# A kernel's first microseconds: fewer zeros, another order of loads and scales, identities scaled in place of weights

## The chip, the cores and the metric

The kernel runs on one core of one Trainium2 chip. A core has five engines that run beside each other and wait for each other by semaphores: TensorE (PE, matmuls; its weight loads are shown apart as PEld), VectorE (DVE), ScalarE (ACT), GpSimd (POOL), and SyncE (SP), which here only issues transfers. ScalarE can issue transfers too. Data lie in SBUF, 128 partitions wide; matmuls write to PSUM, from where VectorE and ScalarE read. The metric is the device time of one execution in microseconds, as a median of several runs. The profiler records one further execution, instruction by instruction; times in it are counted from the start of its span.

## The reference, cut to what matters

Four convolution layers over a signal of 128 samples, 64 channels and 1024 positions, each with weights that are scaled per sample ("modulated") and normalised ("demodulated"). The second layer upsamples and blurs, the fourth blurs and downsamples. The result is added to the input.

```python
CIN, COUT, K, STYLE_DIM = (64, 64, 3, 128)
TYPES = ('same', 'upsample', 'same', 'downsample')
SCALE = 1.0 / sqrt(CIN * K ** 2);  EPS = 1e-08
BLUR_K = [1, 3, 3, 1] / 8

def _layer(x, style, w, b, mw, mb, typ):
    s = style @ mw.T + mb
    weight = SCALE * w * s[:, None, :, None]
    demod = rsqrt(sum(weight * weight, axis=(2, 3)) + EPS)
    weight = weight * demod[:, :, None, None]
    if typ == 'same':       out = conv_same(x, weight) + b
    elif typ == 'upsample': out = blur(conv_up(x, weight) + b, 2 * BLUR_K, (1, 1))
    elif typ == 'downsample': out = conv_down(blur(x, BLUR_K, (2, 2)), weight) + b
    return out

out = x
for i, typ in enumerate(TYPES):
    out = _layer(out, style, weights[i], biases[i], mod_w[i], mod_b[i], typ)
return x + out
```

## The kernel before, in words

All numbers are 32-bit floats. No layer is run over the signal by itself. For every sample the four layers are folded into one filter of nine taps (64 x 64 channels each), and this filter is run over the input. Samples are treated four at a time, a *quad*; there are 32 quads, two samples in the upper and two in the lower 64 partitions. The filter of a quad is made by TensorE in three stages: stage 1 (`stage1`, L410; matmuls by `tap_matmul`, L392) multiplies w2 with w3, scaled per sample (the tiles `wd`, made by `scale3`); stage 2 (`stage2`; matmuls at L553 or L470) multiplies that with E, the blurred w1; stage 3 (L585) multiplies with w0. Between the stages ScalarE or VectorE copy PSUM to SBUF and scale by tables per sample: `S` by tB after stage 1, `R` by tC after stage 2, `Wf` by t0 after stage 3. Then the convolutions over the input run (`product`, L767); their sums are scaled to outputs and stored.

The order of the instructions is written out by hand: each engine executes its instructions in the order in which the program names them, and waits where an operand isn't ready. The scheduler is off. A short prologue, from L1135 on, comes ahead of the loop over quads, and its order is what is changed.

What the prologue does. The parameters come in two arrays: `par_s` with the modulation weights, the styles and the biases, in two parts (the first has layers 2 and 3 and the first 16 samples; the second has layers 0 and 1 and the other samples), and `par` with the weights of the convolutions, copied into the upper and the lower 64 partitions (`HALF`). `par` begins with w2 (KC = 192 columns), then w1 reversed (`w1r`) and a 64 x 64 identity (`idn`), 256 columns together, up to `cuts[1]`; then w3 and w2 in another order up to `cuts[2]`; then the rest. SyncE issues all transfers but two, which ScalarE issues. A transfer is issued in the order of its queue. Behind the parameters, SyncE issues the input of quad 0 (`load(0)`, tile X).

VectorE sets a tile Z to zero, and TensorE multiplies zeros into the two banks of the PSUM tile Y (`zeros_to_y`, L183). These banks are opened that way, and the blur of w1 adds to them. Then `mod_matmul` (L207) multiplies styles with the modulation weights, `mod_scale` (L213) makes `sc`, the scale of each sample and channel, `mod_square` its square `ssq`, `q2_sum` (L228, L229) the sum of the squared weights over taps, and `var_matmul` (L235) the sum under the root. `var_root` (L248, L252) takes the reciprocal root on ScalarE and the sum on VectorE; `newton` (L258 to L260) refines the root in three operations on VectorE. This is done first for layer 2 (`first_inverse`, giving `d2`), which `table_A` needs for the table tA that scales `wd`, and later for all layers (`rest_of_scales`, giving `dm`, from which tC is made).

The blur of w1: `blur_scale` (L320) makes four scaled copies of w1 in the tile `w1s` on ScalarE, one for each distinct value of the seven blur coefficients; `blur_matmul` (L339) multiplies them with the identity and adds them, shifted, into Y; there are 18 matmuls in five steps, taps with 192, 192, 192, 128 and 64 columns in the longer of the two halves. `blur_copy` (L352) copies Y to E.

`load`, `in_g01`, `in_g2`, `in1`, `in2`, `in3` and `in04` (VectorE or GpSimd) form sums and differences of the input. `weight_sums`, `scaled_weights` and the tables tB and t0 run on GpSimd. `ps_conv`, `ps_w` and `ps_y` are the PSUM pools; the modulation's tiles psM lie in `ps_conv`, and the second quad's stage 1 takes the place of the first of them.

Of the kernel before, what the change touches and what calls it, by code (L numbers as in the profile page):

```python
# [63 lines left out]
def kernel(  # L64
# [46 lines left out]
    nc.scalar.dma_start(par[T, :KC], params[:, :KC])  # L111
    nc.sync.dma_start(par_s[:, PS:], params_s[:, PS:])
    nc.scalar.dma_start(par[Bo, : cuts[1]], params[:, : cuts[1]])
    nc.sync.dma_start(par[T, KC : cuts[1]], params[:, KC : cuts[1]])
    for i, j in zip(cuts[1:], cuts[2:]):
        for rows in HALF:
            nc.sync.dma_start(par[rows, i:j], params[:, i:j])
# [32 lines left out]
    Z = const.tile([P, 384], F32, name="Z")  # L150
    E = const.tile([P, NT, C], F32, name="E")
    w1s = const.tile([P, K + 1, K, C], F32, name="w1s")
    nc_v.memset(one, 1.0)
    nc_v.memset(Z[:, :256], 0.0)
    nc_v.memset(Z[:, 256:], 0.0)
# [3 lines left out]
    load(0)  # L159

# [16 lines left out]
    def zeros_to_y(sets, n, start=True):  # L177


        for i in range(sets):  # L180
            rows = HALF[i % 2]
            for cols in HALF:
                nc.tensor.matmul(  # L183
                    Y[cols, i % 2, :n],
                    Z[rows, :C],
                    Z[rows, :n],
                    start=start,
                    stop=True,
                    skip_group_check=not start,
                )  # L190
# [35 lines left out]

    def q2_sum(ls):
# [34 lines left out]
    def first_inverse(bs, src):  # L262

        var_root(bs, src, slice(2, 3), d2[:, None], nc_v)
        newton(var[:, 2, bs], d2, n2)
# [52 lines left out]
    def blur_scale(ks):  # L318
        for i in ks:
            nc_a.activation(w1s[:, i], w1r, AF.Copy, scale=BLUR2[i])  # L320

    def blur_matmul(ps, ks):
# [10 lines left out]
        for k in ks:  # L333
            for r, rows in enumerate(HALF):
# [3 lines left out]
                for cols in HALF:  # L338
                    nc.tensor.matmul(  # L339
                        ps[r][cols, C * (i - lo) : C * (j - lo)],  # L340
                        idn[rows],
                        w1s[rows, min(b, n - 1 - b), i - b : j - b],
# [795 lines left out]
    zeros_to_y(2, 96, False)  # L1138
    nc_v.tensor_scalar_mul(mbs, mb, SCALE)
    mod_matmul(first, pm[0][0], (2, 3))  # L1140
    nc_a.activation(wsq[T, 2], wio[2][T], AF.Square)
    blur_scale(range(2))
    mod_matmul(first, pm[1][0], (0, 1))
    zeros_to_y(2, 128, False)
    mod_scale(first, pm[0][0], slice(2, 4))
    mod_square(first, L2)
    q2_sum(L2)
    var_matmul(first, pm[0][1], (2,))
    mod_scale(first, pm[1][0], L01)
    mod_square(first, L01)  # L1150
    mod_square(first, L3)
    table_B(first)
    table_0(first)
    first_inverse(first, pm[0][1])
    blur_scale(range(2, 4))
    nc_a.activation(wsq[T, 3], wio[3][T], AF.Square)
    blur_matmul(psB, range(5))
    table_A(first, d2)
    scale3(0, BOTH)
# [13 lines left out]
    in_g01(0, PAIR[0])  # L1173
    scale3(1)
    scale3(2)

    def rest_of_scales():
        var_root(first, pm[0][1], eng=nc_v)
# [477 lines left out]
```

## Time and profile before

| | |
|---|---|
| median of 3 runs | 478.26 us (476.77 to 479.97) |
| the profiled execution | 477.31 us, its span 475.5 us |
| granted TensorE clock in it | 0.998 |
| TensorE busy | 469.0 us, 99% of the span |
| VectorE, ScalarE, GpSimd busy | 418.3, 310.6, 163.2 us |
| first zero matmul, first load of the blur, of stage 1, of stage 2 | 1.36, 5.10, 7.51, 10.28 us |

How to read it. In the timeline a line gives the start in us, the length, the engine, the line of the program, the operation, output and inputs, and how many instructions of that kind were merged; behind it, in brackets, how long the engine was idle before and what ended that. `x16` at TensorE counts two records for each matmul of 32-bit floats. In the chain of work that ended last each step is followed back to what released it. Queues are marked with a q (SPq, ACTq). A mean over the 475 us says nothing of the first 14; these are read from the timeline.

### The profile page before, as it was taken

To read this page: it belongs to the slowest core of one execution; us is meant where nothing else is said; L and a number is where in the kernel's file an instruction comes from. 1 tells how busy PE (TensorE), PEld (TensorE's weight loads), DVE (VectorE), ACT (ScalarE), POOL (GpSimd) and SP (SyncE) were. 2 spreads that over 40 slices of the span, in tenths; PEclk is the share of its full clock that TensorE was granted. 3 is DMA by queue.
4 is the path that set the end of the run, shared out by engine and by line. 5 is a ranking of instruction groups with operands and counts; after the bars stand their busy time and mean duration, and the time that the engine had idled before them with its cause. 6 is when DMAs were issued, how large, how long until landed. Compare 5 with 4: busy or idle time off the path is not lost.

```text
span 475.5 us, 26756 instructions
## 1 busy us (share of the span) xinstructions
PE 469.0 (99%) x11928; PEld 351.4 (74%) x11928; DVE 418.3 (88%) x693; ACT 310.6 (65%) x709; POOL 163.2 (34%) x197
## 2 busy tenths in 40 slices
PE   8999999999999999999999999999999999999996
PEld 7986788776778877677776677766777788767863
DVE  4889998879989998999979899979999999999895
ACT  5475666668766676766657666667666768766443
POOL 3534032663534342233432233422334432333200
PEclk9999999999999999999999999999999999999999
DMA  5237455545445554345553455544555554455125
GB/s 176 78 108 222 152 160 170 152 132 167 142 139 174 153 177 127 126 145 174 158 156 128 124 167 152 174 128 125 149 175 157 165 157 144 145 145 176 64 91 193
DMA packets 52243, 70.71 MB, mean 149 GB/s; under 512 B 5856, under 2 KB 49824, under 8 KB 52128
## 3 DMA queue, kind: packets, MB, share of 16 engines
q1 hardware_dynamic: 51536, 68.32, 46.4%
q8 instruction: 93, 1.52, 1.4%
q10 hardware_dynamic: 592, 0.69, 0.5%
q14 instruction: 22, 0.18, 0.1%
HBM read 35.36 MB, written 33.62 MB: 145 GB/s over the span
## 4 chain that ended last, share of the span: by engine, by line
PE 94%; DVE 4%; issue 1%; ACT 0%; ACTq 0%; DVEq 0%
PE psA L767 45%; PE Y L767 11%; PE psR L470 9%; PE psA L585 7%; PE psW L585 7%; PE psS L392 5%; PE psR L553 4%; PE psA L470 2%; PE Y L1008 2%; PE Y L339 1%; DVE H L676 1%; PE Y L183 1%; DVE T L754 1%; DVE G L676 0%; PE psM L207 0%
## 5 line engine op out<-in xcount | busy, mean ns | idle before, releaser
L767 PE MATMUL psA<-T,H 64*64 64x340 f32 x2304 | 186.1, 446 | 0.2 <-DVE y L676 0.2
L767 PEld LDWEIGHTS psA<-T,H 64*64 64x64 f32 x2304 | 91.5, 133 | 46.7 <-issue 2.1
L676 DVE SCALAR_TENSOR_TENSOR G<-X 128x1376 f32<-128x1376 f32 (+2 forms) x65 | 78.4, 1212 | 0.2
L740 POOL TENSOR_TENSOR T<-G 128x684 f32<-128x684 f32 x28 | 46.5, 1659 | 74.1 <-DVE G L676 74.1
L448 POOL TENSOR_TENSOR S<-S 128x128 f32<-128x128 f32 x28 | 21.8, 778 | 139.5 <-ACT S L363 132.2
L363 ACT ACTIVATE R<-psR,tC 128x448 f32<-128x448 f32 x63 | 36.6, 631 | 44.7 <-PE psR L470 26.5
L767 PE MATMUL psA<-T,Wf 64*64 64x340 f32 x768 | 64.0, 446 | 0.0
L767 PE MATMUL Y<-T,Wf 64*64 64x340 f32 x768 | 62.6, 451 | 0.1
L676 DVE SCALAR_TENSOR_TENSOR Y<-m,psA 128x340 f32<-128x340 f32 x64 | 33.0, 516 | 27.6 <-PE psA L767 26.2
L363 ACT ACTIVATE psW<-psA 128x128 f32<-128x128 f32 x100 | 19.3, 268 | 49.2 <-PE psA L585 45.1
L754 DVE TENSOR_TENSOR T<-G 128x1368 f32<-128x1368 f32 (+1 forms) x33 | 50.8, 1541 | 0.0
L363 ACT ACTIVATE Wf<-psW,t 128x256 f32<-128x256 f32 (+2 forms) x76 | 32.7, 480 | 26.5 <-PE psW L585 25.6
L725 DVE TENSOR_TENSOR T<-X 128x684 f32<-128x684 f32 x32 | 48.4, 1513 | 0.0
L470 PE MATMUL psR<-S,E 64*64 64x64 f32 (+1 forms) x1472 | 46.9, 237 | 0.0
L745 POOL TENSOR_TENSOR T<-G 128x684 f32<-128x684 f32 x28 | 46.5, 1660 | 0.0
L392 PEld LDWEIGHTS psS<-wd,w2n 64*64 64x64 f32 x1120 | 34.6, 133 | 12.9
L470 PEld LDWEIGHTS psR<-S,E 64*64 64x64 f32 x1472 | 39.5, 134 | 4.9 <-ACT psR L493 0.2
L767 PEld LDWEIGHTS Y<-T,Wf 64*64 64x64 f32 x768 | 30.2, 132 | 17.1 <-DVE Y L676 0.6
L844 ACT ACTIVATE o<-psA,tb,td 128x340 f32<-128x340 f32 x63 | 37.1, 648 | 6.3 <-PE psA L767 6.3
L767 PEld LDWEIGHTS psA<-T,Wf 64*64 64x64 f32 x768 | 30.2, 133 | 13.9
L844 ACT ACTIVATE o<-Y,tb,td 128x340 f32<-128x340 f32 x63 | 36.7, 639 | 4.5 <-PE Y L767 2.7
L844 ACT ACTIVATE o<-y,tb,td 128x340 f32<-128x340 f32 x62 | 38.6, 679 | 0.6 <-DVE y L826 0.6
(165 smaller groups left out, 832.9 us busy)
## 6 DMA issues: line engine op xcount, KB each, us to landing
out<-o SPq DMA_DIRECT2D x185, 170.0 KB, 2.8
X<-in_x SPq DMA_DIRECT2D x150, 172.0 KB, 3.5
X<-in_x SPq DMA_DIRECT2D x14, 516.0 KB, 5.0
out<-o SPq DMA_DIRECT2D x2, 340.0 KB, 2.8
Xe<-in_x_ends SPq DMA_DIRECT2D x1, 512.0 KB, 5.2
out<-o ACTq DMA_DIRECT2D x3, 170.0 KB, 2.7
par<-in_params SPq DMA_DIRECT2D x2, 192.0 KB, 3.6
par<-in_params SPq DMA_DIRECT2D x2, 96.0 KB, 2.6
```

Source lines behind the costliest of these rows:

```text
L363: nc_a.activation(dst, src, AF.Copy, scale=f)
L392: nc.tensor.matmul(ps[r][cols, at * C : (at + n) * C], weight[rows], wd[c if r == 0 else 1 - c][rows, taps], start=first, stop=last, skip_ ...
L448: nc_g.tensor_add(t[:, :, 2], t[:, :, 2], t[:, :, 0])
L470: nc.tensor.matmul(dst[r][cols], weight[rows], st[c if r == 0 else 1 - c][rows, slots, :], start=False, stop=last, skip_group_check=True,)
L585: nc.tensor.matmul(dst[r][cols], weight[rows], t[rows, c, slots, :], start=first, stop=last, skip_group_check=True,)
L676: nc_v.scalar_tensor_tensor(out, x, f, y, op0=ALU.mult, op1=op)
L725: nc_v.tensor_sub(t[:, pairs, 0, :NJ], plane(X, 3, pairs), plane(X, 1, pairs))
L740: eng.tensor_add(t[:, :, 0, :NJ], plane(g, 2), plane(g, 1))
L745: eng.tensor_sub(t[:, :, 1, :NJ], plane(g, 2), plane(g, 1))
L754: nc_v.tensor_sub(t[:, pairs, :, :NJ], both(a, PL), both(b, 1))
L767: nc.tensor.matmul(ps[s][cols, :NB], w, Ts[q, tag][rows, c, i, g : g + NB], start=(g == 0 and m == 3), stop=(g == K - 1), skip_group_check ...
L844: nc_a.activation(dst, src, AF.Identity, bias=add, scale=d3)
```

## The change

Five things, all in the prologue.

- The transfers: w1 and the identity go second and third in SyncE's queue, both halves; then w3 and the other w2; then the second part of `par_s`; then the rest. ScalarE issues only the upper half of w2. The lower half of w2 goes behind the input of quad 0.
- Z has 64 columns instead of 384 and is set first; the zero matmuls read it repeatedly. The second set of zeros has 128 columns instead of 96.
- The modulation matmuls of layer 2, layer 3 and layers 0 and 1 go in three calls; layer 2's scale is made by itself, and its sum of squared weights by one reduction (`q2_first`). Layers 0 and 1 go between the second and the third step of the blur. `newton_of` reads the sum from PSUM and adds EPS within its first operation.
- The blur multiplies w1 by four scaled identities (`idb`, 64 columns each, made by VectorE) instead of scaled copies of w1 by an identity.
- The roots of all layers, their Newton steps and tC come directly behind quad 0's S, ahead of `wd` of quads 1 and 2 and of quad 0's `in_g01`; `var` is made after them (`first_var`).

```diff
     nc.scalar.dma_start(par[T, :KC], params[:, :KC])
+    for rows in HALF:
+        nc.sync.dma_start(par[rows, KC : cuts[1]], params[:, KC : cuts[1]])
+    for rows in HALF:
+        nc.sync.dma_start(par[rows, cuts[1] : cuts[2]], params[:, cuts[1] : cuts[2]])
     nc.sync.dma_start(par_s[:, PS:], params_s[:, PS:])
-    nc.scalar.dma_start(par[Bo, : cuts[1]], params[:, : cuts[1]])
-    nc.sync.dma_start(par[T, KC : cuts[1]], params[:, KC : cuts[1]])
-    for i, j in zip(cuts[1:], cuts[2:]):
-        for rows in HALF:
-            nc.sync.dma_start(par[rows, i:j], params[:, i:j])
+    for rows in HALF:
+        nc.sync.dma_start(par[rows, cuts[2] :], params[:, cuts[2] :])
...
-    Z = const.tile([P, 384], F32, name="Z")
+    Z = const.tile([P, C], F32, name="Z")
     E = const.tile([P, NT, C], F32, name="E")
-    w1s = const.tile([P, K + 1, K, C], F32, name="w1s")
+    idb = const.tile([P, K + 1, C], F32, name="idb")
+    nc_v.memset(Z, 0.0)
     nc_v.memset(one, 1.0)
-    nc_v.memset(Z[:, :256], 0.0)
-    nc_v.memset(Z[:, 256:], 0.0)
     nc_v.memset(eps, EPS)
 
     nc_a.activation(one, one, AF.Abs_reciprocal_sqrt)
     load(0)
+    nc.sync.dma_start(par[Bo, :KC], params[:, :KC])
...
-                    Y[cols, i % 2, :n],
-                    Z[rows, :C],
-                    Z[rows, :n],
+                    Y[cols, i % 2, :n].rearrange("c (a o) -> c a o", o=C),
+                    Z[rows],
+                    Z[rows, None, :].to_broadcast([C, n // C, C]),
...
+    def q2_first():
+        nc_v.tensor_reduce(
+            q2[T, 2],
+            wsq[T, 2].rearrange("i k o -> i o k"),
+            axis=mybir.AxisListType.X,
+            op=ALU.add,
+        )
...
-    def first_inverse(bs, src):
-
-        var_root(bs, src, slice(2, 3), d2[:, None], nc_v)
-        newton(var[:, 2, bs], d2, n2)
+    def newton_of(src, y, n):
+        nc_v.scalar_tensor_tensor(n, src, EPS, y, op0=ALU.add, op1=ALU.mult)
+        nc_v.scalar_tensor_tensor(n, n, -0.5, y, op0=ALU.mult, op1=ALU.mult)
+        nc_v.scalar_tensor_tensor(y, n, 1.5, y, op0=ALU.add, op1=ALU.mult)
+
+    def first_inverse(bs, ps, ls, y, n):
+
+        src = by_layer(ps, bs)[:, ls]
+        nc_a.activation(y, src, AF.Abs_reciprocal_sqrt, bias=eps)
+        newton_of(src, y, n)
+
+    def first_var(bs, ps):
+        nc_v.tensor_scalar(var[:, :, bs], by_layer(ps, bs), EPS, None, op0=ALU.add)
...
-    def blur_scale(ks):
-        for i in ks:
-            nc_a.activation(w1s[:, i], w1r, AF.Copy, scale=BLUR2[i])
+    def blur_scale():
+        for i in range(K + 1):
+            nc_v.tensor_scalar(idb[:, i], idn, BLUR2[i], None, op0=ALU.mult)
...
-                        idn[rows],
-                        w1s[rows, min(b, n - 1 - b), i - b : j - b],
+                        idb[rows, min(b, n - 1 - b)],
+                        w1r[rows, i - b : j - b],
...
     zeros_to_y(2, 384)
-    zeros_to_y(2, 96, False)
+    zeros_to_y(2, 128, False)
     nc_v.tensor_scalar_mul(mbs, mb, SCALE)
-    mod_matmul(first, pm[0][0], (2, 3))
+    mod_matmul(first, pm[0][0], (2,))
+    mod_matmul(first, pm[1][0], (3,))
     nc_a.activation(wsq[T, 2], wio[2][T], AF.Square)
-    blur_scale(range(2))
+    zeros_to_y(2, 128, False)
+    mod_scale(first, pm[0][0], L2)
+    mod_square(first, L2)
+    q2_first()
+    var_matmul(first, pm[0][1], (2,))
+    mod_scale(first, pm[1][0], L3)
+    blur_scale()
+    blur_matmul(psB, range(2))
     mod_matmul(first, pm[1][0], (0, 1))
-    zeros_to_y(2, 128, False)
-    mod_scale(first, pm[0][0], slice(2, 4))
-    mod_square(first, L2)
-    q2_sum(L2)
-    var_matmul(first, pm[0][1], (2,))
+    blur_matmul(psB, range(2, 5))
+    first_inverse(first, pm[0][1], L2, d2[:, None], n2[:, None])
+    table_A(first, d2)
+    scale3(0, BOTH)
     mod_scale(first, pm[1][0], L01)
+    table_B(first)
+    table_0(first)
     mod_square(first, L01)
     mod_square(first, L3)
-    table_B(first)
-    table_0(first)
-    first_inverse(first, pm[0][1])
-    blur_scale(range(2, 4))
     nc_a.activation(wsq[T, 3], wio[3][T], AF.Square)
-    blur_matmul(psB, range(5))
-    table_A(first, d2)
-    scale3(0, BOTH)
     for l in range(2):
         nc_a.activation(wsq[T, l], wio[l][T], AF.Square)
     blur_copy(psB, (nc_a, nc_a))
...
     stage1(0, None, BOTH, rest_of_var)
-    in_g01(0, PAIR[0])
+    first_inverse(first, pm[0][1], slice(0, NL), dm[:, :, first], nw[:, :, first])
+    table_C(first, nc_v)
     scale3(1)
     scale3(2)
-
-    def rest_of_scales():
-        var_root(first, pm[0][1], eng=nc_v)
-        var_newton(first)
-        table_C(first, nc_v)
-
-    stage2(0, None, BOTH, rest_of_scales)
+    first_var(first, pm[0][1])
+    in_g01(0, PAIR[0])
+    stage2(0, None, BOTH)
```

## The prediction, made before the changed kernel ran

> **What bounds the kernel now.** First the page of the profile: the span, the busy shares, the granted clock by slices, and the chain that ended last by engines.
>
> ```profile
> span 475.5 us, 26756 instructions
> ## 1 busy us (share of the span) xinstructions
> PE 469.0 (99%) x11928; PEld 351.4 (74%) x11928; DVE 418.3 (88%) x693; ACT 310.6 (65%) x709; POOL 163.2 (34%) x197
> ...
> PEclk9999999999999999999999999999999999999999
> ...
> PE 94%; DVE 4%; issue 1%; ACT 0%; ACTq 0%; DVEq 0%
> ```
>
> TensorE (PE) is busy 99% of the span and is 94% of the chain. What the change does to other engines counts only where it moves the moment at which TensorE gets its next work. All edits lie in the first 14 us. So the second view is the timeline of that stretch, TensorE's weight loads alone (start, length, line, count): where a group starts, its matmuls could go.
>
> ```profile
> 1.35 0.30 PEld L183 LDWEIGHTS Y<-Z 64*64 64x64 f32 x8 [1.35 <-DVE eps L156]
> 2.05 0.25 PEld L183 LDWEIGHTS Y<-Z 64*64 64x64 f32 x4 [0.39 <-issue]
> 2.69 0.25 PEld L183 LDWEIGHTS Y<-Z 64*64 64x64 f32 x4 [0.39 <-issue]
> 3.16 0.93 PEld L207 LDWEIGHTS psM<-par_s 128*64 128x64 f32 x16 [0.22 <-issue]
> 4.13 0.31 PEld L183 LDWEIGHTS Y<-Z 64*64 64x64 f32 x8
> 4.66 0.29 PEld L235 LDWEIGHTS psM<-ssq,q 64*64 64x64 f32 x4 [0.22 <-DVE q L229]
> 5.10 2.64 PEld L339 LDWEIGHTS Y<-w1s,par 64*64 64x64 f32 x36
> 7.51 1.86 PEld L392 LDWEIGHTS psS<-wd,par 64*64 64x64 f32 x48
> 9.29 0.43 PEld L235 LDWEIGHTS psM<-ssq,q 64*64 64x64 f32 x12
> 9.75 0.39 PEld L207 LDWEIGHTS psM<-par_s 128*64 128x64 f32 x8
> 10.28 2.42 PEld L553 LDWEIGHTS psR<-S,E 64*64 64x64 f32 x72
> 12.97 0.39 PEld L207 LDWEIGHTS psM<-par_s 128*64 128x64 f32 x8 [0.28 <-issue]
> 13.51 1.09 PEld L392 LDWEIGHTS psS<-wd,par 64*64 64x64 f32 x48
> ```
>
> Read downwards: zero matmuls (L183), the modulation (L207), the sum of squares of layer 2 (L235), the blur of w1 (L339), the first quad's stage 1 (L392), its stage 2 (L553), the second quad's stage 1. From 5.10 on one group follows the other. The blur takes 7.51 - 5.10 = 2.41 us and sets the start of stage 1. Two more facts stand here. Before the blur there are holes, and the modulation lies in them. And the same 48 loads of L392 take 1.86 us at 7.51 but 1.09 at 13.51: TensorE is slow at first, though the granted clock is full.
>
> Third, what releases the blur and stage 1: ScalarE's timeline.
>
> ```profile
> 4.68 0.61 ACT L320 ACTIVATE w1s<-par 128x192 f32<-128x192 f32 x2 [0.96 <-DMA par<-in_params]
> 5.21 0.26 ACT L248 ACTIVATE d<-psM,eps 128x16 f32<-128x16 f32 x1
> ...
> 6.70 0.46 ACT L363 ACTIVATE wd<-par,tA 128x192 f32<-128x192 f32 x1 [0.48 <-DVE tA L290]
> ...
> 11.43 0.30 ACT L248 ACTIVATE dm<-psM,eps 128x64 f32<-128x64 f32 x1
> 13.23 0.64 ACT L363 ACTIVATE R<-psR,tC 128x448 f32<-128x448 f32 x1 [1.50 <-DVE tC L290]
> ```
>
> The blur waits for w1: ScalarE idles 0.96 us on the transfer until 4.68, then scales. Stage 1's weights wd are done at 6.70 + 0.46 = 7.16, which is 0.35 before TensorE is through the blur. So the blur starts stage 1, not the chain of d, tA and wd. Last, SyncE's queue (SPq) and the view of the DMAs (KB each, us from issue to landing).
>
> ```profile
> 0.73 0.38 SPq L110 DMA_DIRECT2D par_s<-in_params_s  x1
> 1.17 0.42 SPq L112 DMA_DIRECT2D par_s<-in_params_s  x1
> 1.63 0.57 SPq L114 DMA_DIRECT2D par<-in_params  x1
> 2.25 2.53 SPq L117 DMA_DIRECT2D par<-in_params  x4
> 4.83 15.99 SPq L146 DMA_DIRECT2D X<-in_x  x4
> ```
>
> ```profile
> par<-in_params SPq DMA_DIRECT2D x2, 96.0 KB, 2.6
> ...
> par_s<-in_params_s SPq DMA_DIRECT2D x1, 120.0 KB, 2.3
> par<-in_params ACTq DMA_DIRECT2D x1, 112.0 KB, 2.8
> par_s<-in_params_s SPq DMA_DIRECT2D x1, 76.0 KB, 1.9
> par<-in_params SPq DMA_DIRECT2D x1, 64.0 KB, 3.0
> ```
>
> w1's upper half is the 64 KB: 1.63 + 3.0 = 4.63, the last to land ahead of 4.68.
>
> **The change, part by part.**
>
> *Fewer zeros.*
>
> ```profile
> 0.80 0.06 DVE L153 MEMSET one<- 128x1 f32 x1 [0.80 <-PEq L1637]
> 0.89 0.27 DVE L154 MEMSET Z<- 128x256 f32 x1
> ```
>
> The new memset of 64 columns costs between nothing and this 0.27; a quarter of the columns would be 0.07 and there is some fixed cost, so I take 0.12. Z now comes first, at 0.80, so TensorE starts near 0.97 instead of 1.35. Its second set of zeros grows from 96 to 128 columns; 384 columns took 2.69 - 1.41 = 1.28, so 32 more are at most 0.1; I take 0.05. The modulation stood behind the zeros, not behind its data (par_s landed at 0.73 + 1.9 = 2.63), so it goes from 3.16 to about 2.83.
>
> *Layer 2's scale first.* The first scale needs two matmuls fewer: 16 loads go in pairs in 0.93, about 0.1 a pair, so with the 0.33 it comes some 0.5 earlier. Two additions for q2 become one reduction, which the trace doesn't show. Its bounds are 0.26 and 0.46, by d (16 columns) and wd (192, as many as it reads), both ScalarE's; I take 0.33, nearer to the short one, as it has half the partitions. The sum of squares starts near 4.0 instead of 4.66, and d near 4.45 instead of 5.21. Newton loses one of four operations. But the four identities stand ahead of Newton on VectorE: behind their wait for w1 queue Newton, tA, half of wd, and the scale of layers 0 and 1.
>
> *w1 and the identities.* SyncE now issues: par_s part one at 0.73; w1's upper half at 1.17; its lower half 0.57 and a gap of 0.05 later at 1.79; w3's two half rows at 2.41 and 3.03; par_s part two at 3.66; the rest; X of quad 0 near 5.4; w2's lower half. The upper half lands by 1.17 + 3.0 = 4.17. The lower half lands between 1.79 + 1.9 = 3.7 and 1.79 + 3.0 = 4.8; I take 4.4, by the 2.6 of the 96 KB in the same queue. The scaling of an identity has 64 columns; w1s took 0.61 for two of 192, so one identity lies between 0.1 and 0.3, and I take 0.2. The blur starts near 4.65, 0.45 earlier. The four identities end near 5.0, Newton, tA and wd follow and end near 6.5, so wd is still not what stage 1 waits for.
>
> The lower half left ScalarE's queue, which issued it beside SyncE's transfers, and is now issued in series. [...]
>
> *What is put into the blur.* The modulation of layers 0 and 1 lay in the hole ahead of the blur and cost nothing. Now it stands between the blur's second and third tap, and needs par_s part two, which is issued at 3.66 instead of 1.17. It lands at 3.66 + 2.3 = 5.96, between 5.6 (1.9) and 6.7 (3.0). In the longer of the blur's halves the taps have 192, 192, 192, 128 and 64 columns, so the first two are half of it, 1.2 us: they end at 4.65 + 1.2 = 5.85. TensorE waits until 5.96. The detour itself: from L207's first load at 3.16 to the next group's at 4.13 are 0.97 for eight pairs of loads; with four pairs 0.57, and with the 0.22 idle ahead of them 0.79. The wait covers that 0.22 here, so 0.57 counts. The blur's other half is 1.2 again: stage 1 starts at 5.96 + 0.57 + 1.2 = 7.73 instead of 7.51. **So 0.45 is gained in front of the blur and about 0.67 is paid inside it: 0.2 later.** An earlier w1 helps no further, since par_s part two is the floor.
>
> *Roots ahead of wd.* dm follows S on ScalarE instead of four wd, so it moves from 11.43 to about 10.3, and tC with it. R's idle of 1.50 on tC shrinks, but that is ScalarE's. R ended at 13.23 + 0.64 = 13.87, while TensorE had the second quad's stage 1 until 13.51 + 1.09 = 14.6. It gains nothing. wd of quads 1 and 2 comes about 0.4 later, near 12, and is wanted at 13.51: no cost.
>
> *The rest.* X is issued 0.6 later; its first user on VectorE now stands behind tC, near 12, 7 us after the issue. The squares of layers 0 and 1 wait for a transfer that is issued 0.6 later, and are wanted by L235 at 9.29 and after. w2's lower half is wanted by GpSimd after stage 2. I cost these at nothing; if the squares' cover fails, the 9.29 group and stage 2 move by up to those 0.6.
>
> **Sum.** Stage 1 starts 0.2 later. If TensorE's change to the quick pace stays where it is, between 7.5 and 10.3, a later stage 1 has more of its loads in the quick time and gives about half back. I take +0.1 on the profiled execution's 477.31 (span 475.5 and 1.8 around it). The median of the three runs, 478.26, is 0.95 above that execution, so the forecast is 478.4, in effect no change. The runs spread from 476.77 to 479.97; about 1% is what a measurement of this kernel can tell from no change.
>
> **Rivals.**
>
> *Quick pace sooner (faster).* TensorE gets dense work 0.4 earlier, and the pace may change before stage 1 or even the blur. Stage 1 at the quick pace saves 1.86 - 1.09 = 0.77, the blur by the same ratio 2.41 x 0.41 = 1.0; at most 1.8, and 1.4 with the 0.2 lost and half of a blur slow: 477.0. For it: the early holes shrink. Against: the detour is a new hole. [...]
>
> *Late par_s and a later pace (slower).* par_s part two now has 64 + 64 + 96 + 96 KB issued ahead of it in one queue. If it lands at 6.7, stage 1 starts at 6.7 + 0.57 + 1.2 = 8.5, 1.0 later. If the longer hole also delays the quick pace past stage 2, that one's 2.69 (10.28 to 12.97) become 2.69 x 1.7 = 4.6. The price is +1.0 to +1.9, I take 1.4: 479.7. It decides from a landing past about 6.2. For it: the queue. Against: 120 KB took 2.3 with ScalarE's transfer beside it.
>
> *The change does what its order says (a little faster).* w1 lands at 3.7, the blur starts at 4.0, par_s part two lands at 5.6: stage 1 at 5.6 + 0.57 + 1.2 = 7.4, 0.1 earlier: 478.2. All landings would have to be short together.
>
> **How the numbers follow.** Forecast 0.5, quick pace sooner 0.2, late par_s 0.2, short landings 0.1. The cases lie between 477.0 and 479.7 with their ends at 476.5 and 480.2; with some 0.4 for the spread of a median the range is 476.1 to 480.6. One per cent is 4.8 us, more than any case gives: faster 0.02, same 0.94, slower 0.04.
>
> **What the changed profile would show.** Zero matmuls from about 0.97; the first scale near 3.3; the blur's first load near 4.65; the modulation of layers 0 and 1 inside the blur near 6.0; stage 1's first load near 7.7; dm near 10.3; stage 2 near 10.4. I am wrong if stage 1's first load stands before 7.3 or after 8.1, if the loads turn quick in another group, or if TensorE waits for S, R or the squares longer than now.

## The result and the profile after

The changed kernel has a median of 478.37 us (22 executions, 476.92 to 480.61); the kernel before, beside it, 477.56 us (22 executions, 476.44 to 479.97). The ratio is 1.0021 with the interval 1.0011 to 1.0031: slower by 0.2%, well inside the 1% that the prediction called no change. (Ratios here are the recorded ones, not quotients of the two medians; the two can differ by up to 0.1%. The quotient here is 1.0017.) The forecast of 478.4 us met the median. The profile shows that it met it for partly other reasons.

The executions of the changed kernel fall into two groups. Six of 22 are above 479.0 us, with a mean of 480.08; the other 16 have a mean of 478.00. Before has one of 22 above 479.0, and a mean of 477.58 without it. So most executions cost 478.00 - 477.58 = 0.42 us more, and about a quarter cost some 2 us on top of that. The profiled execution, 480.31 us with a span of 478.5, is one of the long ones. First its page: span, busy shares, granted clock, chain.

```profile
span 478.5 us, 26754 instructions
...
PE 472.6 (99%) x11928; PEld 349.2 (73%) x11928; DVE 418.1 (87%) x695; ACT 309.7 (65%) x705; POOL 164.1 (34%) x197
...
PEclk9999999999999999999999999999999999999999
...
PE 93%; DVE 4%; issue 1%; SPq 1%; DMA 0%; ACT 0%; ACTq 0%; DVEq 0%
```

TensorE is still 99% of the span and 93% of the chain, and its granted clock is still shown as full in every slice (what the first of these digits are worth is told in the last section). What is new is 1% of SyncE's queue in the chain. The timeline of TensorE's weight loads (start, length, line, count) shows where.

```profile
0.98 0.30 PEld L184 LDWEIGHTS Y<-Z 64*64 64x64 f32 x8 [0.98 <-DVE eps L156]
...
2.90 0.51 PEld L208 LDWEIGHTS psM<-par_s 128*64 128x64 f32 x8 [0.33 <-DMA par_s<-in_params_s]
3.44 0.31 PEld L184 LDWEIGHTS Y<-Z 64*64 64x64 f32 x8
4.06 0.29 PEld L244 LDWEIGHTS psM<-ssq,q 64*64 64x64 f32 x4 [0.32 <-DVE q L229]
4.45 0.94 PEld L357 LDWEIGHTS Y<-par,idb 64*64 64x64 f32 x16
6.10 0.51 PEld L208 LDWEIGHTS psM<-par_s 128*64 128x64 f32 x8 [0.71 <-DMA par_s<-in_params_s]
6.65 1.36 PEld L357 LDWEIGHTS Y<-par,idb 64*64 64x64 f32 x20
7.79 2.15 PEld L410 LDWEIGHTS psS<-wd,par 64*64 64x64 f32 x48
9.81 0.76 PEld L244 LDWEIGHTS psM<-ssq,q 64*64 64x64 f32 x12
10.61 0.67 PEld L208 LDWEIGHTS psM<-par_s 128*64 128x64 f32 x8
11.55 4.40 PEld L571 LDWEIGHTS psR<-S,E 64*64 64x64 f32 x72 [0.28 <-ACT wd L381]
16.23 0.39 PEld L208 LDWEIGHTS psM<-par_s 128*64 128x64 f32 x8 [0.28 <-issue]
16.77 1.09 PEld L410 LDWEIGHTS psS<-wd,par 64*64 64x64 f32 x48
```

Read against the rows of before: the blur (now L357) starts at 4.45 instead of 5.10, 0.65 earlier. Inside it TensorE's weight loads stand 0.71 us on the transfer of par_s, and stage 1 (L410) starts at 7.79 instead of 7.51, 0.28 later. The larger difference comes behind that. Stage 1's 48 loads take 2.15 instead of 1.86, stage 2's 72 (L571) 4.40 instead of 2.42, and the second quad's stage 1 starts at 16.77 instead of 13.51. These 3.26 us are the difference of the spans (3.0) and a little more: nothing further is lost. TensorE keeps its slow pace until 15.7, nearly the end of stage 2; in before it had left it at 9.0, within stage 1.

SyncE's queue tells why par_s comes when it does; one row of the chain in order of time tells when it lands.

```profile
0.73 0.38 SPq L110 DMA_DIRECT2D par_s<-in_params_s  x1
1.18 1.21 SPq L113 DMA_DIRECT2D par<-in_params  x2
2.43 1.24 SPq L115 DMA_DIRECT2D par<-in_params  x2
3.72 0.58 SPq L116 DMA_DIRECT2D par_s<-in_params_s  x1
```

```profile
3.72 2.35 DMA par_s<-in_params_s
```

It is issued at 3.72, behind four half rows at some 0.6 us of issue each, and lands at 3.72 + 2.35 = 6.07. The modulation starts at 6.10. Last, ScalarE's and VectorE's rows that the prediction had named:

```profile
4.51 0.28 ACT L279 ACTIVATE d<-psM,eps 128x16 f32<-128x16 f32 x1 [1.20 <-DVE idb L338]
5.81 0.45 ACT L381 ACTIVATE wd<-par,tA 128x192 f32<-128x192 f32 x1 [1.03 <-DVE tA L308]
...
8.06 0.62 ACT L1181 ACTIVATE wsq<-par 64x192 f32<-64x192 f32 x2 [1.54 <-DMA par<-in_params]
...
10.73 0.31 ACT L279 ACTIVATE dm<-psM,eps 128x64 f32<-128x64 f32 x1
```

```profile
3.35 0.18 DVE L214 SCALAR_TENSOR_TENSOR sc<-psM,mbs 128x16 f32<-128x16 f32 x1 [0.43 <-PE psM L208]
...
3.65 0.36 DVE L229 TENSOR_REDUCE q<-wsq 64x64 f32<-64x192 f32 x1
...
4.20 0.50 DVE L338 TENSOR_SCALAR idb<-par 128x64 f32<-128x64 f32 x4
```

wd is done at 5.81 + 0.45 = 6.26, long before 7.79. The squares of layers 0 and 1 wait 1.54 for their weights, but are done at 8.68, ahead of L244 at 9.81.

### The profile page after: what moved, and what is told of

Read it like the earlier page. It is cut to its first block, busy times and chain, and to the rows that moved or that the text cites. A ratio compares the mean times of both kernels' runs of the same rounds, so it can differ in the third digit from the quotient of the medians.

```text
span 478.5 us, 26754 instructions
## 1 busy us (share of the span) xinstructions
PE 472.6 (99%) x11928; PEld 349.2 (73%) x11928; DVE 418.1 (87%) x695; ACT 309.7 (65%) x705; POOL 164.1 (34%) x197
## 3 DMA queue, kind: packets, MB, share of 16 engines
q8 instruction: 93, 1.52, 1.4%
## 4 chain that ended last, share of the span: by engine, by line
PE 93%; DVE 4%; issue 1%; SPq 1%; DMA 0%; ACT 0%; ACTq 0%; DVEq 0%
PE psA L785 44%; PE Y L785 11%; PE psR L488 9%; PE psA L603 7%; PE psW L603 7%; PE psS L410 6%; PE psR L571 5%; PE psA L488 2%; PE Y L1026 2%; DVE H L694 1%; DVE T L772 1%; DMA par_s<-in_params_s 0%; DVE G L694 0%; PE psM L208 0%; DVE y L844 0%
## 5 line engine op out<-in xcount | busy, mean ns | idle before, releaser
L785 PEld LDWEIGHTS psA<-T,H 64*64 64x64 f32 x2304 | 89.5, 133 | 48.6 <-issue 2.5
L410 PEld LDWEIGHTS psS<-wd,w2n 64*64 64x64 f32 x1120 | 34.8, 133 | 12.8
```

Source lines behind the costliest of these rows:

```text
L410: nc.tensor.matmul(ps[r][cols, at * C : (at + n) * C], weight[rows], wd[c if r == 0 else 1 - c][rows, taps], start=first, stop=last, skip_ ...
L785: nc.tensor.matmul(ps[s][cols, :NB], w, Ts[q, tag][rows, c, i, g : g + NB], start=(g == 0 and m == 3), stop=(g == K - 1), skip_group_check ...
```

## The experiments

Three theories stood against each other. *Later start* (the sum of the prediction): stage 1 is 0.2 to 0.3 later, that is all, and the long executions are chance. *Hole*: the stop inside the blur breaks a dense stretch of TensorE's work, and with it the moment at which its loads turn quick comes later, in some executions by several us. *Roots*: the new order on ScalarE holds stage 2. Below, "long" counts executions above 479.0 us; the kernel before has 9 of 138 over all runs. Ratios are to before on the same chip.

**The changed kernel again.** No edit.

> The changed kernel once more, for a second profile and for the share of its slow executions. Theory 'hole': again a quarter of the executions above 479.0 (6 of 22 before), the others around 478.1; stage 1's first load at 7.7 to 7.8 in the profile whatever the moment of the quick pace. Rival 'chance': the share falls to that of before, 5 of 57, and the ratio to 1.0005 to 1.0010, which is the later stage 1 alone.

Median 478.69 against 477.21, ratio 1.0035 (1.0019 to 1.0051), 5 of 12 long. Its profiled execution, 479.77 us, is long too, and again stage 2 is the slow group (timeline of the weight loads):

```profile
11.46 3.71 PEld L571 LDWEIGHTS psR<-S,E 64*64 64x64 f32 x72 [0.28 <-ACT wd L381]
15.45 0.39 PEld L208 LDWEIGHTS psM<-par_s 128*64 128x64 f32 x8 [0.28 <-issue]
```

So the changed kernel has 11 long executions of 34, and both of those seen in a profile show the same slow group.

**Roots behind wd again.**

```diff
     stage1(0, None, BOTH, rest_of_var)
-    first_inverse(first, pm[0][1], slice(0, NL), dm[:, :, first], nw[:, :, first])
-    table_C(first, nc_v)
+    in_g01(0, PAIR[0])
     scale3(1)
     scale3(2)
-    first_var(first, pm[0][1])
-    in_g01(0, PAIR[0])
-    stage2(0, None, BOTH)
+    def rest_of_scales():
+        first_inverse(first, pm[0][1], slice(0, NL), dm[:, :, first], nw[:, :, first])
+        table_C(first, nc_v)
+        first_var(first, pm[0][1])
+    stage2(0, None, BOTH, rest_of_scales)
```

> The changed kernel with the roots of all layers put back behind the stage 1 weights of quads 1 and 2 and behind the first sums of the input, as before. Theory 'hole': nothing changes, ratio 1.0015 to 1.003 against before, as the changed kernel's 1.0021. Rival 'the rest': ratio back to 1.000 to 1.001 if the new order of the roots costs, or 1.003 to 1.004 if it gains.

Median 477.98 against 477.32, ratio 1.0023 (1.0005 to 1.0040), 3 of 11 long: as the changed kernel. The order of the roots costs and gains nothing that shows. As TensorE's order is that of the changed kernel, the two together have 14 long executions of 45 (31%), against 9 of 138 (7%) before. The profiled execution here is a short one, 477.73 us:

```profile
7.75 1.93 PEld L410 LDWEIGHTS psS<-wd,par 64*64 64x64 f32 x48
...
10.59 2.41 PEld L571 LDWEIGHTS psR<-S,E 64*64 64x64 f32 x72
...
13.82 1.10 PEld L410 LDWEIGHTS psS<-wd,par 64*64 64x64 f32 x48
```

Stage 1 starts where it does in the long execution (7.75 and 7.79), yet stage 2 takes 2.41. The start of stage 1 alone does not decide the group to which an execution belongs.

**The modulation ahead of the blur, its transfer second in the queue.** (par_s part two is issued directly behind ScalarE's first transfer.)

```diff
     mod_matmul(first, pm[1][0], (3,))
+    mod_matmul(first, pm[1][0], (0, 1))
...
-    blur_matmul(psB, range(2))
-    mod_matmul(first, pm[1][0], (0, 1))
-    blur_matmul(psB, range(2, 5))
+    blur_matmul(psB, range(5))
```

> The changed kernel with two edits taken back: par_s part two is second in SyncE's queue again, and the modulation of layers 0 and 1 goes ahead of the blur, which is then in one piece. Theory 'hole' (the modulation inside the blur delays stage 1, and its hole breaks the only long dense stretch of TensorE's work, so that the quick pace comes later in many executions): stage 1's first load near 7.3 (blur from about 4.9, 2.4 long), under the 7.51 of before, and times as those of before or up to 0.5 us shorter, ratio 0.999 to 1.000, with at most one execution in ten above 479.2. Rival 'chance' (the moment of the quick pace is drawn alike for all kernels, and only the start of stage 1 counts): also ratio about 0.9995, but with as many executions above 479.2 as the changed kernel has, 6 of 22. Rival 'the rest' (what costs is the order of the roots or the new scalings): stays at 1.002.

Median 477.57, ratio 1.0006 (0.9992 to 1.0021), 2 of 11 long (479.19 and 479.34). The blur starts at 4.94 and stage 1 at 7.35, which is 0.16 before the kernel before has it. No loss is clear of noise any more, though the interval overlaps that of the changed kernel, and no gain came in its place: what is won in front of the blur, 0.16 here, is too little to be measured.

**The whole blur first, the modulation behind it.** The queue's order stays that of the change.

```diff
-    blur_matmul(psB, range(2))
+    blur_matmul(psB, range(5))
     mod_matmul(first, pm[1][0], (0, 1))
-    blur_matmul(psB, range(2, 5))
```

> The changed kernel with the modulation of layers 0 and 1 behind the whole blur instead of within it; the queue's order stays. The wait for par_s part two (6.07 to 6.10) then falls into the blur's own time, and only the detour is left. Theory 'hole': blur from 4.45 to about 6.9, stage 1's first load near 7.5, 0.25 earlier than the changed kernel; most executions 0.2 to 0.4 shorter, ratio 1.000 to 1.0015; the dense stretches (2.4 for the blur, 2 for stage 1) are still apart, so executions above 479.0 remain at one in ten to one in four. If the wait were all that costs, the ratio would be 0.9995 to 1.0005 and slow executions as rare as before.

```profile
4.46 2.64 PEld L357 LDWEIGHTS Y<-par,idb 64*64 64x64 f32 x36
7.22 0.51 PEld L208 LDWEIGHTS psM<-par_s 128*64 128x64 f32 x8
7.76 1.73 PEld L410 LDWEIGHTS psS<-wd,par 64*64 64x64 f32 x48
...
10.39 2.39 PEld L571 LDWEIGHTS psR<-S,E 64*64 64x64 f32 x72
...
13.60 1.10 PEld L410 LDWEIGHTS psS<-wd,par 64*64 64x64 f32 x48
```

Median 477.89, ratio 1.0013 (1.0000 to 1.0025), 0 of 11 long, the highest 478.62. This is the cleanest comparison. Stage 1 starts at the same place as in the changed kernel (7.76 and 7.79), the same matmuls run, and only the stop inside the blur is gone; with it the long executions go. At the changed kernel's share of 31%, none of 11 would be a chance of 2%. Only the long executions go: the mean here is 477.91, and on the same chip the seven executions of the changed kernel that are not long have a mean of 477.87, against 477.17 for such executions of before. One execution in ten to one in four was expected to stay long. The start of stage 1 was expected at 7.5 and missed: the detour costs 7.76 - (4.46 + 2.41) = 0.89, not 0.57. So the wait for par_s in the changed kernel (0.93 in all) was nearly covered by what the detour costs anyway, and the harm of the stop is not its length.

**The stop alone, in the kernel before.** The modulation of layers 0 and 1 is put between the second and third tap there, with its data long landed; the scale and table work that hangs on it goes behind `scale3(0, BOTH)`.

```diff
-    mod_matmul(first, pm[1][0], (0, 1))
...
-    blur_matmul(psB, range(5))
+    blur_matmul(psB, range(2))
+    mod_matmul(first, pm[1][0], (0, 1))
+    blur_matmul(psB, range(2, 5))
```

> The kernel before with one edit: the modulation of layers 0 and 1 moved between the second and the third step of the blur (and the scale that follows it put behind stage 1's weights). Its data have landed long before, so there is no wait, only the detour. Theory 'hole': stage 1's first load 0.55 to 0.7 later than 7.51, so 8.1 to 8.2, and times 0.8 to 1.5 us above before, ratio 1.002 to 1.003, a quarter or more of the executions above 479.2. Rival 'chance': the detour alone, ratio 1.0006 to 1.0014, and executions above 479.2 as rare as before. Rival 'the rest': ratio 1.000 to 1.001.

```profile
6.60 0.51 PEld L207 LDWEIGHTS psM<-par_s 128*64 128x64 f32 x8 [0.54 <-issue]
7.14 1.36 PEld L339 LDWEIGHTS Y<-w1s,par 64*64 64x64 f32 x20
8.28 2.15 PEld L392 LDWEIGHTS psS<-wd,par 64*64 64x64 f32 x48
...
14.62 1.10 PEld L392 LDWEIGHTS psS<-wd,par 64*64 64x64 f32 x48
```

Median 478.37, ratio 1.0018 (1.0002 to 1.0035), 2 of 11 long, with only one above 479.2. Stage 1 comes 0.77 later than before and takes all of its loads slow; stage 2 is quick. The time is lost, but a quarter of long executions was expected and did not come. The weight loads idle 0.54 here with no transfer behind it, against 0.71 in the changed kernel.

**Zero matmuls in the same place of the kernel before**, so that the blur is split but TensorE kept busy.

```diff
-    blur_matmul(psB, range(5))
+    blur_matmul(psB, range(2))
+    zeros_to_y(2, 384, False)
+    blur_matmul(psB, range(2, 5))
```

> The kernel before with four more zero matmuls of 384 columns in the same place, between the second and the third step of the blur: about the same length as the detour (0.64 us by the 1.28 that four such matmuls take in two passes, less if they overlap), but with TensorE dense. Nothing is left out of the computation; zeros are added. Theory 'hole': stage 1 0.6 to 1.3 later, yet no more executions above 479.2 than before apart from that shift, and the quick pace in the profile at the latest near 9.5; ratio 1.0005 to 1.0015. Rival 'chance': the same ratio as the kernel with the detour if stage 1 starts at the same time. The two differ in what the pair of kernels shows: with 'hole' the one with the detour is slower than this one, with 'chance' it is not.

```profile
8.59 1.13 PEld L392 LDWEIGHTS psS<-wd,par 64*64 64x64 f32 x48
...
13.86 1.10 PEld L392 LDWEIGHTS psS<-wd,par 64*64 64x64 f32 x48
```

Median 478.06, ratio 1.0011 (0.9993 to 1.0028), 1 of 12 long. Stage 1 starts at 8.59, 0.31 after that of the run above, but its loads are quick at once (1.13 us for 48), and the second quad's stage 1 follows at 13.86 instead of 14.62. In these two profiles a busy filling gives back the time that a stop loses. In the medians it is inconclusive: 0.3 between the two runs, with intervals that overlap. The spans of the same executions say more. In this run alone the time is up to 3.7 us longer than the span (1.7 to 1.9 in all others, for a reason that isn't known); its one long execution, 479.70, has a span of 476.0. The median spans are 475.5 for before, 475.95 here and 476.6 with the modulation in this place. That speaks for the filling, with 12 and 11 executions.

**More zeros from the start, in the kernel before.** Z is set first and read with a broadcast, as in the change, and the second set has 256 columns.

```diff
-    zeros_to_y(2, 96, False)
+    zeros_to_y(2, 256, False)
```

> The kernel before with the small Z set first, and its second set of zeros of 256 columns instead of 96, so that TensorE works without a hole from 0.98 to the modulation at about 3.2, where it stood before. The path behind it is not touched: stage 1's first load at 7.5. Theory 'hole' (the quick pace follows a dense stretch): if 2.2 us of zeros in one piece, with the modulation and further zeros behind them, are dense enough, the quick pace comes before 8.5 in some executions, and times fall by 0.3 to 0.8 us, ratio 0.998 to 0.9995; if the modulation's small matmuls (3.2 to 4.1) break it as the hole in the blur does, nothing changes: 0.9995 to 1.0005. Rival 'chance': 0.9995 to 1.0005.

Median 477.34, ratio 1.0000 (0.9987 to 1.0014), 0 of 11 long. Zeros from 0.98, a blur at 4.94: no gain.

**The same 256 columns with the modulation ahead of the blur** (on top of the changed kernel with the modulation ahead of the blur).

```diff
-    zeros_to_y(2, 128, False)
+    zeros_to_y(2, 256, False)
```

> The changed kernel with the modulation of layers 0 and 1 ahead of the blur (as in the run with that edit, which began stage 1 at 7.35) and the second set of zeros of 256 columns, so that TensorE is dense from 0.98 to about 3.2. The modulation starts 0.3 later, which stage 1's weights can take (they were ready 0.9 ahead of it). Theory 'hole': stage 1's first load at 7.35 to 7.5, few executions above 479.0, ratio 0.998 to 1.000, and below the kernel before if the longer zeros bring the quick pace sooner. Rival 'chance': 0.9995 to 1.0005.

Median 477.33, ratio 1.0009 (0.9998 to 1.0020), 0 of 12 long: above the range of either theory, but not clear of 1. These two and the run with the modulation ahead of the blur have no stop inside it, and all three stand within 0.1% of before.

**par_s part two third in the queue**, behind w1's halves and ahead of w3's; the modulation stays inside the blur.

```diff
+    nc.sync.dma_start(par_s[:, PS:], params_s[:, PS:])
     for rows in HALF:
         nc.sync.dma_start(par[rows, cuts[1] : cuts[2]], params[:, cuts[1] : cuts[2]])
-    nc.sync.dma_start(par_s[:, PS:], params_s[:, PS:])
```

> The changed kernel with one edit: par_s part two goes directly behind w1's two halves, ahead of w3's two half rows, so that it lands near 2.43 + 2.3 = 4.8 instead of 6.1. The modulation stays inside the blur. Theory 'hole': no wait, the detour alone; blur from 4.45, first half 1.35 with its drain, detour 0.55, so stage 1's first load at 7.4 to 7.55, 0.2 to 0.35 earlier than the changed kernel; the hole is a third shorter, so slow executions (above 479.0) fall below the changed kernel's 14 of 45 but may stay above before's 7 of 92; ratio 1.0005 to 1.0015. If only the wait counted, the ratio would be 0.9995 to 1.0005. If neither (the rest of the change), 1.002 to 1.0035.

```profile
5.81 0.51 PEld L208 LDWEIGHTS psM<-par_s 128*64 128x64 f32 x8 [0.54 <-issue]
6.36 1.36 PEld L357 LDWEIGHTS Y<-par,idb 64*64 64x64 f32 x20
7.49 1.67 PEld L410 LDWEIGHTS psS<-wd,par 64*64 64x64 f32 x48
...
12.74 0.19 PEld L208 LDWEIGHTS psM<-par_s 128*64 128x64 f32 x3 [0.28 <-issue]
13.30 0.33 PEld L208 LDWEIGHTS psM<-par_s 128*64 128x64 f32 x5 [0.37 <-issue]
```

Median 477.06 against 476.87, ratio 1.0006 (0.9992 to 1.0019), 1 of 12 long. No transfer is waited for. The split alone still costs 7.49 - (4.33 + 2.41) = 0.75, and with the 0.77 gained in front of the blur stage 1 is where it was before. The long executions come with the split and the late transfer together; the split with 0.54 of idle makes few or none (3 of 35, with the run below that has X later and the stop put into before). Stage 2 starts at 10.08, the earliest so far, but the second quad's stage 1 at 13.78 is not earlier than before: a hole of 0.37 stands in the middle of eight loads of one line, with nothing that they wait for.

**A long set of zeros** (512 columns, on top of the run with the modulation ahead of the blur), to make the loads turn quick as early as can be.

```diff
-    zeros_to_y(2, 128, False)
+    zeros_to_y(2, 512, False)
```

> The changed kernel with the modulation of layers 0 and 1 ahead of the blur and the second set of zeros of 512 columns, so that TensorE runs zeros without a hole from 0.98 to about 4.1, 3.1 us. The modulation starts near 4.2 and the blur near 5.7, 0.8 later than with 256 columns, so stage 1 would start near 8.1 at the slow pace. Theory 'hole' (the quick pace follows a dense stretch of some 3.4 us): part of the executions turn quick between 4.4 and 6, ahead of the blur, and are then as fast as before or up to 0.5 faster; the others lose up to 0.8, half of it given back; the spread of the times widens, ratio 0.999 to 1.0015. Rival 'chance' (the moment doesn't depend on what TensorE does): ratio 1.0008 to 1.0017, all executions alike.

```profile
4.13 0.55 PEld L208 LDWEIGHTS psM<-par_s 128*64 128x64 f32 x16 [1.56 <-issue]
...
5.38 1.39 PEld L357 LDWEIGHTS Y<-par,idb 64*64 64x64 f32 x36
7.34 1.10 PEld L410 LDWEIGHTS psS<-wd,par 64*64 64x64 f32 x48 [0.58 <-ACT wd L381]
...
9.73 2.38 PEld L571 LDWEIGHTS psR<-S,E 64*64 64x64 f32 x72
12.39 0.19 PEld L208 LDWEIGHTS psM<-par_s 128*64 128x64 f32 x3 [0.28 <-issue]
14.28 0.33 PEld L208 LDWEIGHTS psM<-par_s 128*64 128x64 f32 x5 [1.70 <-issue]
```

In this execution the loads are quick from 4.13: the modulation's 16 take 0.55 instead of 0.93, the blur's 36 take 1.39 instead of 2.64. The quick pace came here after zeros without a stop from 0.98; it does not always, as the run with X later shows. That a stretch of some 3.4 us of dense work brings the quick pace, as the theory has it, is shown by no run: from the start of the work without a stop to the quick pace it is at most 4.13 - 0.98 = 3.15 here, 9.02 - 5.10 = 3.92 in before, and in the changed kernel the 15.72 - 6.10 = 9.62 behind the stop, with one idle of 0.28 in it. The median is 477.60 against 476.87, ratio 1.0017 (1.0002 to 1.0032), 1 of 12 long: above the theory's range, at the upper end of the rival's. How many of the 12 turned quick so early is not known. In the profiled one the gain is lost again. First, stage 1 now waits 0.58 for wd. Then stage 2 starts 0.55 ahead of before, and a hole of 1.70 us takes it back: between the third and fourth load of the same group as above. The view of the DMAs shows, in the window 11.9 to 12.0, and not in 3.0 to 11.9, a packet of the queue that it lists as `q8 instruction`:

```profile
q8 instruction: 1, 0.02, 60.1%
```

Before has this packet in 9.4 to 9.5, the changed kernel in 10.4 to 10.5, the run with par_s third at about 10.96. From packet to end of the hole it is 14.28 - 11.94 = 2.34 here, and 13.30 - 10.96 = 2.34 there, at the same instruction. In before, in the changed kernel and in the two runs with X later (packets at 9.4, 10.4, 9.4 and 9.2) 2.34 us behind the packet lies ahead of the moment at which TensorE comes to this group (12.97, 16.23, 13.68 and 13.35), and none of the 12 profiles beside the two has the hole. What TensorE stands on in the hole the profile doesn't name; that it is its code is the author's estimate from these times and from two shares: q8 carries 1.52 of the 1.70 MB of instruction packets, 89%, and 23,856 of the 26,756 instructions traced in before, 89%, are TensorE's.

**X's second half issued later**, behind the squares' sums, to let that packet come sooner; once on top of the long zeros, once on top of par_s third.

```diff
-    load(0)
+    nc.sync.dma_start(Xs[0][:, 0, :], x[0])
...
     q2_sum(L01)
+    nc_v.memset(Xs[0][:, 1:2, 0:1], 0.0)
+    nc.sync.dma_start(Xs[0][:, 1, :], x[1])
```

> The kernel with the long zeros, and the second half of quad 0's X is issued only when VectorE has summed the squares (near 9) instead of at about 6. In the run with the long zeros TensorE stood 1.70 us at 12.5 in the middle of four equal weight loads, waiting for nothing that the profile shows, while the first 16 KB packet of TensorE's instructions went out at 11.94, behind X. Theory 'code' (TensorE's next instructions are fetched over the same transfer engines and come late behind X): the packet goes out near 9.5 to 10.5, the hole of 1.70 is gone or under 0.5, and in an execution that is quick early stage 1 of quad 1 starts near 13 instead of 14.75; median 0.3 to 1.2 us shorter than the 477.6 with the long zeros. Rival 'X itself' (the hole waits for something else that this order brings): the hole stays at 1.7 and the time within 0.3.

> The kernel with par_s part two third in the queue, and the second half of quad 0's X issued only behind the sums of the squares. There the hole at the same weight load was 0.37 and the packet went out at 10.96. Theory 'code': the hole is gone, the packet goes out near 9.5 to 10.3; median 0 to 0.4 us shorter than the 477.06 without the edit, as the hole is only there when the quick pace comes before stage 1's end; ratio to before 0.9985 to 1.0005, which would make it the best of the versions. Rival: the hole stays, ratio 1.0000 to 1.0012. If X's later half is itself missed, VectorE waits for it near 13 to 14 and the ratio is above 1.001.

The first of the two profiles, with the same zeros from 0.98:

```profile
4.17 0.93 PEld L208 LDWEIGHTS psM<-par_s 128*64 128x64 f32 x16 [1.61 <-issue]
```

Here the loads are still slow at 4.17, as in all other profiles: of the two profiles with these zeros one has the quick pace early and the other doesn't. Long zeros: median 477.64 against 477.35, ratio 0.9997 (0.9981 to 1.0014), 0 of 12 long. par_s third: 477.78, ratio 1.0006 (0.9994 to 1.0019), 0 of 12. The packet came at 9.4 and 9.2, and neither profiled execution has the hole. But in both the loads turned quick late (9.8), so that TensorE came to the instruction at 13.75 and 13.41; at the old packet times, by the 2.34, an estimate, it would have stood 0.5 us in the first and not at all in the second. Neither the 0.3 to 1.2 us nor the 0 to 0.4 us hoped for is shown: against before on the same chip the first ratio went from 1.0017 to 0.9997, with intervals that overlap, and the second stayed at 1.0006. That X's second half alone sets the packet's time isn't shown either: in before and in the changed kernel, with nothing held back, the packet came at 9.4 and 10.4. No version beats the kernel before by more than its interval.

## Why the prediction was right, and where it was not

- **Front of the blur: right, gain undersized.** Zeros at 0.98 (0.97), first scale 3.35 (3.3), reduction 0.36 (0.33), sum of squares 4.06 (4.0), d 4.51 (4.45). The blur came at 4.45, not 4.65, as w1's 64 KB halves landed in 2.3 each. They were issued at 1.18 and 1.80 and landed at 3.47 and 4.11, as far apart as they were issued; 4.4 had been taken for the second.
- **Paid inside the blur: right.** par_s landed at 6.07 for 5.96: issued at 3.72 for 3.66, and 2.35 long for 2.3. Stage 1 came at 7.79 for 7.73, by the steps that the prediction adds up: the landing, the detour of 0.55 (6.10 to 6.65; forecast 0.57), the second half of 1.14 (forecast 1.2). What is paid inside, 7.79 - 4.45 - 2.41 = 0.93 for 0.67, is larger because the blur started 0.20 earlier and had to wait for par_s all the same, as the prediction says of an earlier w1. Without a wait the split costs 0.75 (par_s third), near the prediction's 0.79 with its idle time; behind the whole blur the detour costs 0.89.
- **Roots, wd, X, squares, w2 at nothing: right.** The run with the roots put back has the changed kernel's time; the squares and wd were in time, and the first uses of X on VectorE (12.48) and of w2's lower half on GpSimd (16.40) don't wait. dm came at 10.73 for 10.3 because TensorE was late, not ScalarE, which stood 0.97 us on stage 1's sums until 10.23.
- **The step that failed is in the Sum:** "If TensorE's change to the quick pace stays where it is ... about half back. I take +0.1". Where the pace does stay, one profile has it right: with the modulation behind the blur stage 1 starts as late as in the changed kernel (7.76), the loads turn quick near 9.1 (before: 9.0), and the second quad's stage 1 is 0.09 later than before (13.60 for 13.51). But the pace does not stay. With the roots put back it came near 9.4, and the same group was 0.31 later. In most executions the loss is 0.42, not 0.1; 14 of 45 lose some 2 more; in the two of these that a profile shows, the quick pace comes only at 14.2 and 15.7 us. Over the 22 executions the means differ by 478.56 - 477.69 = 0.87, about half from each.
- **Its own sign of being wrong came:** "if the loads turn quick in another group". In before they turn in stage 1, in the two long executions in stage 2. Stage 2 started at 11.55 in the first of them, for 10.4.
- **That the number fitted is luck.** The forecast was +0.1 on the median of before; measured are 478.37 - 477.56 = +0.81. The 0.95 added for the median of three runs was too high by about as much: with 22 executions before stands at 477.56, not 478.26.
- **The rival "late par_s and a later pace" is what was seen** in the long executions. Its slow stage 2 was priced right (stage 2 and its successor took 4.68 us, 16.23 - 11.55; forecast 4.6). Its condition was wrong: it was to decide from a landing past 6.2, and the one in the long execution was at 6.07. Its two costs, 1.0 and 1.9, would add to 2.9 where both hold; it took 1.4. The long executions are 480.08 - 477.58 = 2.50 above before. It was given 0.2 as a case apart; 14 of 45 executions are long, so, if they all are what the two profiles show, it is a share of every set of runs.
- **"Quick pace sooner" did not come** in a profile of this change. Its saving of 1.4 does not follow from its terms: 0.77 and half of 1.0, less 0.2, make 1.1. When the loads were quick from 4.13 with the long zeros in one execution, the blur's took 1.39 instead of 2.64 and that execution as a whole gained nothing (478.32 us): the weight loads stood 0.58 on wd and then 1.70 in the hole.
- **Open:** how busy TensorE must be for the pace to change (the last section has what the profiles show); and what the 0.1% of the run with the modulation behind the blur consists of, whose profile shows only 0.09 us of it.

## What to carry to other kernels

A matmul group that waits for a transfer should not stand inside a dense stretch of TensorE's early work: here the stop is paid once as idle time (0.71 us of the weight loads) and, in some executions (14 of 45, against 9 of 138 before), several times over as slow work behind it (4.40 us for stage 2's loads, for 2.42). Before an operand is sent back in a queue, count the issues that it falls behind (here four of 0.6 us each) and look at which engine waits for it first. A prologue's gain is worth only what the next floor leaves of it (with the long zeros the weight loads stood 0.58 us on wd and 1.70 in the hole), and a few executions with a long tail show such a loss before the median does: count them.

## What the runs showed of the hardware that was not expected

The pace of TensorE's weight loads is not in the digits of the granted clock on the page, which are full throughout: one load of 64x64 takes 227 ns slow (the blur's in before) and 133 quick (those of its stage 2), 48 of them 2.15 and 1.09 us. It is in the records behind the digits. The trace keeps the granted clock as stretches with a start and a length, and the first stretch, at full clock, starts within 0.1 us of the moment at which the loads turn quick: at 9.02 us in before, 15.72 in the changed kernel. Ahead of it there is no record, and the page shows 9s there all the same; that TensorE was slow though the granted clock was full, as the prediction has it, is a reading of these 9s. The stretch is 464.21 us long in before and 460.80 in the changed kernel, 136 and 135 times 3.413; what this step comes from is not shown. In the other runs the moment is an estimate from the length of the row into which it falls, between that of a slow and that of a quick one: near 9.1 with the modulation behind the blur, 9.4 with the roots put back, 14.2 in the second profile of the changed kernel, 9.8 in the two runs with X later.

Why one order of instructions has short and long executions is not shown. The stop inside the blur ends at 6.10, 6.02 and 6.07 in the two profiles of the changed kernel and in that with the roots put back, and stage 1 starts at 7.79, 7.70 and 7.75; the quick pace comes at 15.7, 14.2 and 9.4. Nor does TensorE's busy time tell the moments apart. In the 3.41 us ahead of the change it is busy 3.41 in before (5.61 to 9.02) and 3.41 in the changed kernel (12.31 to 15.72), but the two stretches of the same length that precede this one have 3.41 (8.90 to 12.31) and 3.31 (5.48 to 8.90, with the end of the stop), and the loads stay slow. With the long zeros TensorE is busy 3.01 of the first 4.00 us and the loads are quick from 4.13; with X later as well, the same zeros run and they are slow at 4.17. How full a stretch must be, and of what length, no run shows.

The first packet of the queue q8 in the span came at 9.4 us in before, 10.4 in the changed kernel, 9.4 and 9.2 in the two runs with X later, 10.96 with par_s third and 11.94 with the long zeros. In the two with the latest packets TensorE stood 0.37 and 1.70 us between two weight loads of the same line, with no semaphore to wait for, until 2.34 us behind the packet.
